# Weight sums of a Strassen MLP made during attention: 48 pieces of 192 columns in the first 24 chunks, in place of 72 pieces of 128 columns in all 36

## The chip, the cores and the metric

The kernel runs on one core of a Trainium2 chip. The metric is the device time of one execution in microseconds (us), as a median over executions. The core has TensorE (PE, with its weight loads as PEld), VectorE (DVE), ScalarE (ACT), GpSimd (POOL) and SyncE (SP), which here only issues DMAs. POOL also issues DMAs of its own.

## The reference

One image of 48 x 48 tokens with 768 channels goes through a transformer block and then through a Fourier block (AFNO). Cut to what matters here:

```python
xn   = layernorm(x)
qkv  = xn @ qkv_w + qkv_b                        # 12 heads of 64 channels
attn = softmax(q*scale @ k.T + rel_h + rel_w)    # 2304 x 2304 for each head
x    = x + (attn @ v) @ proj_w + proj_b
h    = gelu(layernorm(x) @ mlp_w1 + mlp_b1)      # 3072 hidden channels
x    = x + h @ mlp_w2 + mlp_b2
x    = x + irfft2(blockwise_mlp(rfft2(x)))       # AFNO
```

## The kernel before

All matmuls are in float32. The dense layers are computed in Strassen-Winograd form: a product of two-by-two blocks is made of seven block products instead of eight. For that, sums of the weight blocks are needed. With the blocks a11, a12, a21, a22 of a weight, the helper `left` (L164 to L167) makes four 128 x n sums or differences, three into new tiles and one in place; `right` (L175 to L178) does the same for the other operand. The MLP weights `mlp_w1` and `mlp_w2` are turned into such sets of seven while attention runs, and the results are kept in DRAM (`w1_d`, `w2_d`) until the MLP reads them.

**Attention.** Heads go in pairs (`pr`, 6 of them), queries in chunks of 384 (`c`, 6 of them), so there are 36 chunks. In a chunk, PE makes the scores of 18 key tiles for both heads (`content`, L678, and `position`, L687), ACT takes the exponential into `exps` (L697, tile `main`), DVE adds the exponentials up in `pairs` (L871), then `acc` (L875). Then PE makes the products with the values in six thirds (`products`, L710). Between those thirds the list `between` puts other work:

- third 1: `asked`, then `denominators` on DVE (transpose L728, reduction into `part` L730);
- third 4: `inverses`: PE sums `part` over partitions (L739, one matmul ahead of the rest of the products), DVE takes the reciprocal into `rden` (L741) and adds to `sums` (L742), POOL adds `rden` to `inverse` (L743). `rden` has two buffers;
- third 5: SP stores `rden` to DRAM (`left_apart`, L757), stores earlier outputs (`stored`, L791), reads the denominators back to all partitions (L770). DVE scales the output of the chunk two before (`scaled`, L782, tile `o`, two buffers), and POOL adds the bias of the values to it (L785).

SP also issues 24 small DMAs for each chunk that fill `terms` (L317 and L321), read by L687.

**The weight sums.** `sum_jobs` lists 72 jobs: 12 hidden chunks, two weights, three pieces of 128 columns. A job takes three steps on POOL, all through one tile `seven` with a single buffer:

```python
nc.gpsimd.dma_start(out=seven[:, :4], in_=(w1_blocks, w2_blocks)[k][n, i])   # L802, in asked
(left, right)[k](nc.gpsimd, ...)                                             # four sums, in summed
nc.gpsimd.dma_start(out=to, in_=seven)                                       # L815, in summed
```

`asked` is called twice in a chunk (at key tile 2 and in third 1) and `summed` twice (at key tile 12 and after the chunk's last product), so a chunk takes two jobs and the 72 jobs fill the 36 chunks. As `seven` has one buffer, the load of the next job waits until the store of the one before has landed. POOL works through its instructions in order, so the `inverse` addition and the bias addition of a chunk stand behind the jobs that are ahead of them.

**After attention.** DVE adds up `sums` and `inverse` (L1005, L1006) to a flag that says whether the softmax without a maximum was safe (L1008, L1010; PE turns it with L1028), makes the weight sums of the projection (L919), and then takes the projection's products as they come. The first two token tiles are projected plainly (`plainly`, PE L933, DVE L937), the next ones by seven products (`projected`, PE L957, DVE L970, L975, L979, POOL L967). The sums of the attention output that these need are made on DVE (`ogs`, L175 to L178). POOL adds the bias of the projection to the 18 tiles of the residual (`residual`, L896). Then a branch on the flag (L1044, L1045), the rest of the projection, the MLP (L1320, L1378, reading `w1_d` and `w2_d` at L1302 and L1305), and AFNO.

The order on PE, SP, ACT, DVE and POOL is the written one within each of these stages.

Of the kernel before, what the change touches and what calls it, by code (L numbers as in the profile page):

```python
# [10 lines left out]
F32 = mybir.dt.float32  # L11
# [8 lines left out]
P = 128  # L20
# [7 lines left out]
FF = 4 * C  # L28
FCH = 256
# [5 lines left out]
CH = C // 2  # L35
# [12 lines left out]
def block_then_afno(  # L48
# [27 lines left out]
    nc = tc.nc  # L76
# [18 lines left out]
    dram = ctx.enter_context(tc.tile_pool(name="scratch", bufs=1, space=DRAM))  # L95
# [9 lines left out]
    oT = dram.tile([C, T], F32, name="oT")  # L105
    stat_d = [dram.tile([12, P], F32, name=f"stat_d{p}") for p in range(T // TB)]
    den_d = dram.tile([NC * (T // G), 2 * G], F32, name="den_d")
    w1_d = [dram.tile([P, 7, 3, P], F32, name=f"w1_d{n}") for n in range(FF // FCH)]
    w2_d = [dram.tile([P, 7, FF // (FCH * NS), CH], F32, name=f"w2_d{s}") for s in range(NS)]

    big1 = ctx.enter_context(tc.tile_pool(name="big1", bufs=1))
# [91 lines left out]
    with ExitStack() as flag_scope:  # L203
# [12 lines left out]
        with ExitStack() as att:  # L216
# [444 lines left out]
            with tc.manual_schedule(engines={mybir.EngineType.PE, mybir.EngineType.SP}):  # L661
# [6 lines left out]
                o_pool = att.enter_context(tc.tile_pool(name="att_o", bufs=2))  # L668
# [121 lines left out]
                        pr, c, o = results.pop(0)  # L790
                        queue.dma_start(out=oT[ts(pr, P), ts(c, G)], in_=o)  # L791

                sum_jobs = [(k, n, i) for n in range(FF // FCH) for k in range(2) for i in range(3)]
                in_hand = []

                def asked():

                    if not sum_jobs:
                        return
                    k, n, i = sum_jobs.pop(0)  # L800
                    seven = o_pool.tile([P, 7, P], F32, name="seven", bufs=1)
                    nc.gpsimd.dma_start(out=seven[:, :4], in_=(w1_blocks, w2_blocks)[k][n, i])  # L802
                    in_hand.append((k, n, i, seven))

                def summed():

                    if not in_hand:
                        return
                    k, n, i, seven = in_hand.pop(0)
                    (left, right)[k](  # L810
                        nc.gpsimd, *(seven[:, a] for a in range(4)), [seven[:, a] for a in (4, 5, 6)]
                    )
                    s, j = divmod(n, FF // (FCH * NS))
                    to = w2_d[s][:, :, j, ts(i, P)] if k else w1_d[n][:, :, i]
                    nc.gpsimd.dma_start(out=to, in_=seven)  # L815

                def between(pr, c, acc):

# [28 lines left out]
                with tc.manual_schedule(  # L847
# [4 lines left out]
                    for pr in range(NC):  # L852
                        for c in range(T // G):
# [4 lines left out]
                            if c == 4 and pr == NC - 1:  # L858
                                nc.sync.dma_start(
                                    out=pw, in_=proj_w.rearrange("(c p) f -> p c f", p=P)  # L860
                                )
                            pairs = o_pool.tile([P, 2, 2, G], F32, name="pairs", bufs=1)
                            for kt in range(NT):
                                if kt == 2:
                                    asked()
                                elif kt == 12:
                                    summed()
                                scores(pr, c, kt, exps[:, kt])
                                if kt > 2 and kt % 2:
                                    so_far = exps[:, ds(0, 2)] if kt == 3 else pairs  # L870
                                    nc.vector.tensor_tensor(  # L871
                                        pairs, so_far, exps[:, ds(kt - 1, 2)], ALU.add
                                    )
# [4 lines left out]
                            for i in range(6):  # L878
                                for what in work.get(i, ()):
                                    what()  # L880
                                products(op, heads[pr][2], range(3 * i, 3 * i + 3))
                            finish(pr, c, op)
                            summed()
                    scaled(0)
                    stored(nc.gpsimd)
# [102 lines left out]
        with tc.tile_pool(name="ps_flag", bufs=1, space=PSUM) as psum, tc.tile_pool(  # L988
            name="ps_early", bufs=1, space=PSUM
# [55 lines left out]
        with tc.If(safe < 1):  # L1045
            with ExitStack() as att:
                xnT = main.rearrange("p (c t) -> p c t", c=NC)
                with tc.tile_pool(name="g_ln1", bufs=3) as ln1, tc.tile_pool(
                    name="g_ps_ln1", bufs=2, space=PSUM
# [24 lines left out]
                for pr in range(NC):  # L1074
                    w3 = []
                    for n, name in enumerate(("g_wq", "g_wk", "g_wv")):
                        w = w_pool.tile([P, NC, P], F32, name=name)
                        nc.sync.dma_start(
                            out=w,
                            in_=qkv_w[:, ds(n * C + pr * P, P)].rearrange("(c p) f -> p c f", p=P),  # L1080
# [33 lines left out]
                    for sg in range(T // SG):  # L1114
# [37 lines left out]
                        for i in range(2):  # L1152
                            wp = psum.tile([P, 24, 16], F32, name="g_wp", tag="m")
                            for r in range(24):
                                w = i * 24 + r
# [15 lines left out]
                        for j in range(2):  # L1171
                            for qt in range(SG // P):

                                s = p_pool.tile([P, T], F32, name="s")
# [25 lines left out]
                                for kg in range(NT // 3):  # L1200
# [20 lines left out]
                                    out=oT[ds(pr * P + 64 * j, 64), ds(sg * SG + qt * P, P)],  # L1221
                                    in_=ot[rows, :],
                                )
            with tc.tile_pool(name="g_ps_proj", bufs=2, space=PSUM) as psum, tc.tile_pool(
                name="g_og", bufs=2
# [17 lines left out]
        with tc.tile_pool(name="ps_proj", bufs=1, space=PSUM) as psum, tc.tile_pool(  # L1243
            name="ps_turn", bufs=2, space=PSUM
        ) as psum_turn, tc.tile_pool(name="proj_late", bufs=2) as pl:
            hats, ogs = [], {EARLY: sums_of_outputs(pl, kept[EARLY])}
            for u in range(EARLY, PAIRS):
# [5 lines left out]
                n = u - EARLY  # L1253
# [29 lines left out]
    with ExitStack() as mlp:  # L1283
# [15 lines left out]
        def weights(p, n):  # L1299

            w = wpool.tile([P, 7, 3, P], F32, name="w1")
            nc.sync.dma_start(out=w, in_=w1_d[n])  # L1302
            v = wpool.tile([P, 7, CH], F32, name="w2")
            g, j = divmod(n, FF // (FCH * NS))
            nc.sync.dma_start(out=v, in_=w2_d[g][:, :, j])  # L1305
            ready_w[p, n] = w, v

        def hidden(p, n):
# [29 lines left out]
            nc.scalar.copy(m1, bank[0])  # L1338
            product(1, s2, t2, True)
            u = summed(bank[1], m1, "u")  # L1340
            yield
            product(2, a21, t3, True)
# [93 lines left out]
        def turned(piece):  # L1436

            for i in range(4 * piece, 4 * piece + 4):
# [6 lines left out]
                )  # L1445

        weights(0, 0)
        for p in range(T // TB):
            for n in range(n_f):
                if (p, n) == (0, 2):  # L1450
                    nc.sync.dma_start(out=b2, in_=mlp_b2[0, :].partition_broadcast(P))
                    nc.sync.dma_start(out=rows_dft, in_=c_rows)
                work = hidden(p, n)
                for i in range(3):
                    next(work)
                    if n:
                        added(p, n - 1, i)
                if n < n_f - 1 and (p == 0 or n):
                    weights(p, n + 1)
                if p < 2 and 4 <= n < 10:  # L1460
                    normalised(p + 1, n - 4)
            for i in range(3):
                if p < 2:
                    turned(i)
                added(p, n_f - 1, i)
            if p < 2:
                sums_of_tokens(xt, xs)
                for n in range(2):
                    weights(p + 1, n)
            rows_forward(p)  # L1470
        in_order.close()

    with ExitStack() as sp:
# [35 lines left out]
        for t in range(2):  # L1509
            nc.sync.dma_start(  # L1510
                out=d2[ts(t, HW)].rearrange("p n o -> p (n o)"),
                in_=fb2[t, :].partition_broadcast(HW),
# [272 lines left out]
def _laid_out(x, given):  # L1785

    import numpy as np

    w = {name: np.asarray(a) for name, a in given.items()}

    def columns(v):
        return v.reshape(-1, P).T

    vecs = np.concatenate(
        [
            columns(v)
            for v in (
                w["L0_conv_ln1_g"],
                w["L0_conv_ln1_b"],
                w["L0_conv_ln2_g"],  # L1800
                w["L0_conv_ln2_b"],
                w["L0_conv_qkv_b"],
                w["L0_conv_mlp_b1"],
            )
        ],
        axis=1,
    )

    rel = np.zeros((HD, 2, 112), np.float32)
    for i, name in enumerate(("L0_conv_rel_pos_h", "L0_conv_rel_pos_w")):  # L1810
        rel[:, i, : 2 * HW - 1] = w[name][::-1].T
    n_s, n_j = NS, FF // (FCH * NS)
    arrays = {
        "x": np.asarray(x).reshape(T, C),

        "x_blocks": np.asarray(x).reshape(6, 8, 3, 16, C).transpose(0, 2, 1, 3, 4).reshape(T, C),
        "x_turned": np.asarray(x).reshape(6, 8, 3, 16, C).transpose(4, 0, 2, 1, 3).reshape(C, T),
        "qkv_w": w["L0_conv_qkv_w"],
        "proj_w": w["L0_conv_proj_w"],
        "w1_blocks": w["L0_conv_mlp_w1"]  # L1820
        .reshape(2, 3, P, n_s, 2, n_j, P).transpose(3, 5, 1, 2, 4, 0, 6)
        .reshape(n_s * n_j, 3, P, 4, P),
        "w2_blocks": w["L0_conv_mlp_w2"]
        .reshape(n_s, 2, n_j, P, 2, 3, P).transpose(0, 2, 5, 3, 1, 4, 6)
        .reshape(n_s * n_j, 3, P, 4, P),
        "vecs": vecs,
        "v_b": w["L0_conv_qkv_b"][None, 2 * C :],
        "proj_b": w["L0_conv_proj_b"][None],
        "mlp_b2": w["L0_conv_mlp_b2"][None],
        "rel": rel,  # L1830
        "fw1": w["L1_conv_w1"].transpose(2, 0, 1, 3),
        "fb1": w["L1_conv_b1"].transpose(2, 0, 1),
        "fw2": w["L1_conv_w2"].transpose(2, 1, 0, 3),
        "fb2": w["L1_conv_b2"].reshape(2, -1),
    }
    return {name: np.ascontiguousarray(a) for name, a in arrays.items()}
# [24 lines left out]
```

## Time and profile before

| what | value |
|---|---|
| time, median of 3 runs | 2864.15 us (2859.18 to 2873.69) |
| the profiled execution's own time | 2856.51 us |
| its span, first to last instruction | 2854.7 us |
| mean granted TensorE clock | 0.993 |
| attention: first POOL job to last product | about 403 to 1419 us of the span |
| projection up to the branch | about 1419 to 1503 us |
| busy in 402 to 1420: PE, DVE, ACT, POOL | 1012.91, 697.53, 621.88, 467.34 us |
| busy in 1420 to 1462: PE, DVE, ACT, POOL | 26.57, 17.42, 0.48, 22.61 us |

A row of a group of instructions reads: line, engine, operation, output and input tiles with their shapes, how many; then busy time and mean of one in ns; then idle time of the engine before them and what ended it. A row of the waits reads: engine, tile and line that waited, what released it; then us in total, times, longest. A row of a timeline reads: start, duration, engine, line, operation, tiles, count, and in brackets the idle time before it and what ended that. Times are from the start of the span.

### The profile page before, as it was taken

What the parts mean: (1) busy time and instruction counts of PE and PEld (TensorE: products, weight loads), DVE (VectorE), ACT (ScalarE), POOL (GpSimd) and SP (SyncE); (2) the same over time, 40 slices, a digit from 0 to 9 for tenths busy, and PEclk for the clock granted to TensorE, in tenths of its full rate; (3) what the DMA queues carried; (4) which work ended last, traced back from release to release, by engine and by line L of the source; (5) the groups of instructions that cost most, each with busy time, mean ns of one, the idle gap of its engine ahead of it and who ended that gap; (6) DMA issues with size and microseconds to landing.
All of it is one profiled execution on the core that took longest, in us unless ns stands there. A gap on an engine that the chain in (4) does not pass through costs nothing. (4 is left out here: it accounts for less than half of the span.)

```text
span 2854.7 us, 41104 instructions
## 1 busy us (share of the span) xinstructions
PE 2795.7 (98%) x15759; PEld 1719.4 (60%) x15759; DVE 1719.9 (60%) x2520; ACT 920.0 (32%) x1466; POOL 804.8 (28%) x806
## 2 busy tenths in 40 slices
PE   8999999999999999999989999999999999999999
PEld 4555656665656565656545555555555555556887
DVE  5434246767676676767546665675565566566665
ACT  1101126666656575756401211021011211112332
POOL 3505124444445344444573100020000100002432
PEclk9999999999999999999989999999999999999999
DMA  4535387485875858677453232332232322233254
GB/s 154 177 104 168 101 170 164 105 171 124 145 179 117 173 122 164 139 141 138 136 181 111 75 116 78 116 132 73 111 116 78 141 97 102 92 107 111 61 161 141
DMA packets 233405, 363.47 MB, mean 127 GB/s; under 512 B 26948, under 2 KB 203964, under 8 KB 227056
## 3 DMA queue, kind: packets, MB, share of 16 engines
q1 hardware_dynamic: 215720, 306.80, 40.7%
q0 software_dynamic: 15040, 52.11, 6.1%
q8 instruction: 127, 2.08, 0.3%
q10 hardware_dynamic: 2440, 1.84, 0.2%
q14 instruction: 78, 0.64, 0.1%
HBM read 211.59 MB, written 85.35 MB: 104 GB/s over the span
## 5 line engine op out<-in xcount | busy, mean ns | idle before, releaser
L697 ACT ACTIVATE main<-sp 128x768 f32<-128x768 f32 x648 | 516.4, 812 | 34.5 <-PE sp L687 19.3
L1320 PE MATMUL h<-shared,w 128*128 128x384 f32 x1512 | 504.1, 486 | 0.7 <-issue 0.7
L871 DVE TENSOR_TENSOR pairs<-pairs,main 128x1536 f32<-128x1536 f32 x252 | 456.9, 1813 | 27.1 <-DVE pairs L871 0.9
L687 PE MATMUL sp<-terms,select 64*128 64x384 f32 x1296 | 412.3, 629 | 0.0
L1320 PEld LDWEIGHTS h<-shared,w 128*128 128x128 f32 x1512 | 287.0, 190 | 202.0 <-issue 2.5
L1380 DVE TENSOR_TENSOR main<-o,main 128x384 f32<-128x384 f32 x540 | 299.1, 557 | 38.3 <-PE o L1378 0.2
L1395 POOL TENSOR_TENSOR main<-main,acc 128x384 f32<-128x384 f32 x9 | 11.4, 1263 | 924.5 <-DVE main L1380 665.3
L678 PE MATMUL sp<-shared 64*128 64x384 f32 x1296 | 264.9, 485 | 1.6 <-ACT row_hi L249 1.0
L678 PE MATMUL sp<-qT,kT 64*128 64x384 f32 x1296 | 264.5, 484 | 0.0
L1378 PE MATMUL o<-w,hs 128*128 128x384 f32 x648 | 262.5, 487 | 1.5 <-DVE hs L165 1.0
L1378 PE MATMUL o<-w,hT 128*128 128x384 f32 x648 | 245.1, 487 | 3.0 <-DVE main L1380 3.0
L710 PE MATMUL op<-main,shared 128*64 128x384 f32 x1296 | 218.0, 488 | 0.0
L710 PE MATMUL op<-main,v 128*64 128x384 f32 x1296 | 217.2, 488 | 0.0
L1326 ACT ACTIVATE hT<-c,vec 128x384 f32<-128x384 f32 x108 | 66.5, 615 | 465.1 <-DVE c L1332 465.1
L871 DVE TENSOR_TENSOR pairs<-main 128x1536 f32<-128x1536 f32 x36 | 64.0, 1778 | 221.5 <-ACT main L697 221.4
L1332 DVE TENSOR_TENSOR c<-h,u 128x384 f32<-128x384 f32 x108 | 60.2, 557 | 212.9 <-PE h L1320 212.9
L1378 PEld LDWEIGHTS o<-w,hT 128*128 128x128 f32 x648 | 122.7, 190 | 90.2 <-DVE main L1380 6.3
L1378 PEld LDWEIGHTS o<-w,hs 128*128 128x128 f32 x648 | 122.5, 190 | 89.5 <-DVE main L1380 4.9
L687 PEld LDWEIGHTS sp<-terms,select 64*128 64x128 f32 x1296 | 125.5, 186 | 83.6
L537 PE MATMUL m<-main 128*128 128x384 f32 x504 | 164.2, 487 | 2.1 <-DVE main L187 1.6
L710 PEld LDWEIGHTS op<-main,v 128*64 128x64 f32 x1296 | 97.3, 137 | 92.4 <-issue 67.7
L710 PEld LDWEIGHTS op<-main,shared 128*64 128x64 f32 x1296 | 96.5, 137 | 89.3 <-issue 64.4
(205 smaller groups left out, 3807.3 us busy)
## 6 DMA issues: line engine op xcount, KB each, us to landing
w<-w_d SPq DMA_DIRECT2D x72, 1344.0 KB
w_d<-seven POOLq DMA_DIRECT2D x72, 448.0 KB, 4.6
terms<-col_parts SPq DMA_DIRECT2D x432, 72.0 KB
seven<-in_w_blocks_dram POOLq DMA_DIRECT2D x72, 256.0 KB, 4.4
terms<-row_hi SPq DMA_DIRECT2D x216, 72.0 KB
terms<-row_lo SPq DMA_DIRECT2D x216, 72.0 KB
main<-in_qkv_w_dram SPq DMA_DIRECT2D x36, 384.0 KB
z<-zt SPq DMA_DIRECT2D x48, 192.0 KB
```

The lines of the kernel that those rows point to most:

```text
L537: nc.tensor.matmul(bank, a[:, c, :], b[:, c, :], start=(first and c == 0), stop=(c == 2), skip_group_check=not first,)
L678: nc.tensor.matmul(sp[:, j, :G], kT[at, ts(kt, P)], qT[at, ts(c, G)], start=first, stop=not first,)
L687: nc.tensor.matmul(sp[:, j, :G], select[at, a % 2], ready[pr, c][at, a // 2, b], start=first, stop=not first,)
L697: nc.scalar.activation(p, sp[:, :, :G], AF.Exp, scale=HD**-0.5)
L710: nc.tensor.matmul(op[ts(j, 64)], v[:, kt, ts(j, 64)], exps[:, kt, j, :], start=(kt == 0), stop=(kt == NT - 1),)
L871: nc.vector.tensor_tensor(pairs, so_far, exps[:, ds(kt - 1, 2)], ALU.add)
L1320: nc.tensor.matmul(bank[i], a[:, c, :], b[:, c, :], start=(start and c == 0), stop=(c == 2), skip_group_check=not start,)
L1326: nc.scalar.activation(h[:, i, ts(k, G)], src, AF.Gelu, bias=col(V_B1 + tiles_of_chunk(n)[i]))
L1332: nc.vector.tensor_tensor(t, src, other, ALU.add)
L1378: nc.tensor.matmul(bank[k], a, b, start=start, stop=True, skip_group_check=not start)
L1380: nc.vector.tensor_tensor(dst, bank[k], dst, ALU.add)
L1395: nc.gpsimd.tensor_tensor(x12, x12, acc[i], ALU.add)
```

## The change

A job has 192 columns instead of 128. There are two pieces for each weight chunk instead of three, so 48 jobs; still two in a chunk, so the list is empty after 24 chunks. A load moves 384 KB instead of 256 KB, a store 672 KB instead of 448 KB; the four sums run over 128 x 192 elements. The weights are laid out for that in the input arrays, and `w1_d` is kept as 7 x 384 columns for each partition; the MLP reads the same bytes in the same order as one run per partition. The tile `seven` grows by 7 x 64 x 4 = 1792 bytes per partition.

```diff
-    w1_d = [dram.tile([P, 7, 3, P], F32, name=f"w1_d{n}") for n in range(FF // FCH)]
+    w1_d = [dram.tile([P, 7, CH], F32, name=f"w1_d{n}") for n in range(FF // FCH)]
...
-                sum_jobs = [(k, n, i) for n in range(FF // FCH) for k in range(2) for i in range(3)]
+                sum_jobs = [(k, n, i) for n in range(FF // FCH) for k in range(2) for i in range(2)]
...
-                    seven = o_pool.tile([P, 7, P], F32, name="seven", bufs=1)
+                    seven = o_pool.tile([P, 7, CH // 2], F32, name="seven", bufs=1)
...
-                    to = w2_d[s][:, :, j, ts(i, P)] if k else w1_d[n][:, :, i]
-                    nc.gpsimd.dma_start(out=to, in_=seven)
+                    to = w2_d[s][:, :, j] if k else w1_d[n]
+                    nc.gpsimd.dma_start(out=to[:, :, ts(i, CH // 2)], in_=seven)
...
-            nc.sync.dma_start(out=w, in_=w1_d[n])
+            nc.sync.dma_start(out=w.rearrange("p a c f -> p a (c f)"), in_=w1_d[n])
...
-        .reshape(2, 3, P, n_s, 2, n_j, P).transpose(3, 5, 1, 2, 4, 0, 6)
-        .reshape(n_s * n_j, 3, P, 4, P),
+        .reshape(2, 3, P, n_s, 2, n_j, P).transpose(3, 5, 2, 4, 0, 1, 6)
+        .reshape(n_s * n_j, P, 4, 2, CH // 2).transpose(0, 3, 1, 2, 4),
...
-        .reshape(n_s, 2, n_j, P, 2, 3, P).transpose(0, 2, 5, 3, 1, 4, 6)
-        .reshape(n_s * n_j, 3, P, 4, P),
+        .reshape(n_s, 2, n_j, P, 2, 2, CH // 2).transpose(0, 2, 5, 3, 1, 4, 6)
+        .reshape(n_s * n_j, 2, P, 4, CH // 2),
```

Here P is 128 and CH is 384.

## The prediction

> **What bounds the kernel now.** I read the page first: PE is busy in 98% of the span, POOL in 28%.
>
> ```profile
> PE 2795.7 (98%) x15759; PEld 1719.4 (60%) x15759; DVE 1719.9 (60%) x2520; ACT 920.0 (32%) x1466; POOL 804.8 (28%) x806
> ```
>
> So work taken off POOL gains nothing by itself. What counts is where PE waits, and whether POOL is behind that. The table of waits, read next, has POOL as the releaser in one long wait only, and POOL itself waits mostly for its own DMAs:
>
> ```profile
> POOL seven L802 <- DMA w_d<-seven: 301.2, 71, 8.4
> POOL seven L164 <- DMA seven<-in_w_blocks_dram: 99.6, 31, 9.7
> POOL seven L175 <- DMA seven<-in_w_blocks_dram: 88.0, 33, 5.4
> DVE total L1006 <- POOL inverse L743: 28.3, 1, 28.3
> ```
>
> A job is thus a serial chain (load, wait, four sums, store, wait), and at the end of attention DVE waits 28.3 us for POOL's last `inverse`. The timelines show why: POOL is a chunk late. In chunk 3 of 36, PE's denominator product (L739) is at 481.08 and POOL's `inverse` at 481.84. In the last chunk PE's is at 1414.82, POOL's at 1444.04, a lag of 29 us:
>
> ```profile
> 481.08 0.19 PE L739 MATMUL small<-gather,part 128*48 128x32 f32 x1
> 481.84 0.53 POOL L743 TENSOR_TENSOR inverse<-inverse,rden 24x32 f32<-24x32 f32 x1 [2.23 <-DVE sums L742]
> 1414.82 0.19 PE L739 MATMUL small<-gather,part 128*48 128x32 f32 x1
> 1444.04 0.27 POOL L743 TENSOR_TENSOR inverse<-inverse,rden 24x32 f32<-24x32 f32 x1
> ```
>
> PE pays for this lag after attention, in PE's timeline behind its last product (1414.89 + 4.06 = 1418.95):
>
> ```profile
> 1414.89 4.06 PE L710 MATMUL op<-main,v 128*64 128x384 f32 x23
> 1423.68 18.25 PE L933 MATMUL m<-col_parts,og 128*128 128x384 f32 x48 [4.73 <-DMA og<-oT]
> 1445.63 0.27 PE L1028 MATMUL line<-ident,both 128*1 128x128 f32 x1 [3.69 <-DVE both L1010]
> 1449.62 3.71 PE L957 MATMUL m<-col_parts,og 128*128 128x384 f32 x6 [3.72 <-DVE main L937]
> 1457.67 4.21 PE L957 MATMUL m<-pws,ogs 128*128 128x384 f32 x6 [4.33 <-DVE ogs L176]
> 1461.67 2.73 PE L957 MATMUL m<-col_parts,og 128*128 128x384 f32 x6
> ```
>
> Inside attention PE loses almost nothing today, but with no reserve. DVE ends `part` (L730) at 1413.75 + 0.95 = 1414.70, and PE uses it at 1414.82. A DVE that comes later stops PE.
>
> **What the Trainium skill says.** (1) "SBUF — State Buffer", section "SBUF: two separate sides": a DVE instruction with two SBUF inputs and a POOL instruction that reads SBUF exclude each other for a whole instruction. The trace agrees: a sum of 128 columns takes 443 to 460 ns alone and up to 2.0 us when an L871 addition (1.76 us) is under way, and L871 takes 1.757 us at least, 1.823 in the median. (2) "DMA: Bandwidth & Descriptors", section "Anatomy of one DMA — SWDGE (gpsimd) path": a POOL DMA takes about 2.0 us plus bytes/436e3. For 256 KB this gives 2.6 and for 448 KB 3.05; the trace has at least 2.7 and 3.6, and 4.4 and 4.6 in the median, where DMAs of SP compete. (3) "PSUM — Partial Sum Buffer", section "Engine vs sequencer instructions": queues of POOL and DVE are strict first in, first out. The trace agrees: `inverse`, ready at 1415.4, runs behind the jobs at 1444.04.
>
> **Part 1, a longer job.** Today, from the rows by form: load issue 0.56, wait for the load 187.6/72 = 2.61, four sums 311.0/72 = 4.32, gap 0.40, store issue 0.93, wait for the store 301.2/71 = 4.24: 13.1 us. Two jobs, `inverse` 0.52 and bias 1.34 make 28.0 us a chunk, beside PE's chunk of (1419.01 - 430.14)/35 = 28.25 us (ends of chunks by ACT's copy L751). With waits for DVE (50.7/36 = 1.4) POOL needs slightly more than PE, hence the lag.
>
> With 192 columns:
>
> - Sums: 128 x 384 takes 1130 ns (L164 on `main`), 128 x 128 at least 443, so 2.7 ns a column: 64 columns in four sums add 0.69 us, alone or behind DVE.
> - Load: by the skill's rate at least 131072/436e3 = 0.30; at most half of what lies over the fixed 2.0, (4.4 - 2.0)/2 = 1.2. I take 0.5.
> - Store: at least 229376/436e3 = 0.53, at most (4.6 - 2.0)/2 = 1.3. I take 0.85. Both stand nearer the low end: part of the surplus is waiting in the queue, which bytes do not lengthen. The issues (0.56, 0.93) keep their number of rows; I leave them.
>
> A job gets 2.04 us longer (1.5 to 3.2), so a chunk's POOL work is 28.0 + 4.1 = 32.1 us against 28.25. The lag grows by 3.83 us a chunk, 88 us over the 23 chunks up to the last with jobs.
>
> **How much lag is free.** Behind POOL's jobs stand `inverse` and the bias addition. DVE's L741 of chunk c needs the `rden` buffer of c-2 (two chunks, 56.5 us), and L782 needs an `o` whose bias addition stood in POOL's queue at c-2 and which SP has then stored. Between L741 and the next L871 DVE has 8.3 us (1388.28 to 1396.56), 1.6 of it work, so 6.7 to spare. By `rden` the limit is 56.5 + 6.7 = 63 us. By `o` it is 56.5 + 7.7 - 1.6 for bias and issue - 5.5 for landing (L791 on POOL's queue) = 57. I use 57. Past that DVE starts `pairs` late, `part` is late, and PE waits at L739, with the products and the next chunk's scores behind it. SP, stuck in L791, holds `terms` back as well, but those are issued chunks ahead. The stall is 88 - 57 = **+31 us**. With both ends: 3.2 to a job gives 23 x 6.15 - 57 = 84, and 1.5 gives 23 x 2.75 - 57 = 6.
>
> **Part 2, DVE beside longer sums.** L871 loses 0.066 us to a sum of 128 columns. 64 more hold the port some 0.14 us longer. The mean of a sum, 1.08 us between 0.45 and 1.9, says that some 43% of eight a chunk collide: 0.5 us a chunk on DVE. In about half of 24 chunks there is no reserve: **+4 us** (2 to 8). Gone in the last 12 chunks: under 1 us.
>
> **Part 3, the end.** Without jobs in the last 12 chunks POOL has 1.9 us of work a chunk and catches up at once. `inverse` follows L739 within 1 us as in chunk 3, L1006 runs at about 1416, flag and L919 are done by 1421, and L937 meets each product as it comes. SP's L791, today stuck until 1418.36 for POOL's L785 of 1417.08, goes early, and `og` is there when the last product ends. PE then runs 18.25 us of L933 from 1419, the transpose, two products of 1.94, and stands at 1441.5 where it stands now at 1461.67: **-20 us**. If `og` still arrives at 1423.7, it is -15.5. What is late next: L896, paced by L967 and so by PE, moves along; the wait at the branch (3.89 us) stays.
>
> **Without cost:** the MLP's weight reads (same bytes, same runs), the larger tile, 96 DMA issues instead of 144, 192 sums instead of 288 (POOL is not PE).
>
> **Sum.** 31 + 4 - 20 = +15 us on 2856.51, the profiled execution, 2871.5. Its time lies 7.6 under the median of 2864.15, so **2879 us**.
>
> **Rivals.** *Faster:* the lag stays below 57, there is no stall, and only the end is seen: 4 - 20 = -16, 2848 us. It decides at a job longer by (57/23 + 0.25)/2 = 1.36 us; the sums and the skill's least DMA times already give 1.52, so DMA growth would have to be hidden or the free lag nearer 65. For it speaks that today's POOL held a lag of 30 without cost. *No change:* the job grows by 1.5 to 2.0, the stall is 6 to 29 and mostly cancels the end: 2854 to 2877. *Much slower:* the DMAs grow with bytes in full, +68, 2932. *It does not do what it says:* POOL clears late but the end is bound by SP's reload of the denominators (an 8.9 us wait) and not by POOL; then the end gives little and the stall stays, near 2895.
>
> **Chances.** Within 0.5% (14 us; about what a measurement of this kernel can tell from no change) 0.27; slower 0.50, with the last two rivals in it; faster 0.23. Range 2847 to 2910: from the faster rival to a job 2.7 us longer (stall 61, +45).
>
> **What would show it.** Right: L743's lag behind L739 grows by about 4 us a chunk to some 55 to 60 by chunk 16, then PE waits at L739 for L730 by about 4 us a chunk until chunk 24; chunks 25 to 36 take 28.2 us; L1006 no longer waits; L933 to the third L957 without gaps. Job sums of 0.62 us alone, landings of 4.9 (load) and 5.4 (store). Wrong: the lag levels off under 57 with no waits at L739 (the faster rival), or chunks slow down before the lag is there (DVE beside POOL was underpriced).

## The result and the profile after

The changed kernel takes **2882.3 us** (median of 20 runs, 2871.1 to 2889.3), the kernel before 2864.1 (20 runs beside it, 2855.0 to 2876.8). The ratio is 1.0056 with a 95% interval of 1.0043 to 1.0070: slower by 18 us, where 2879 was forecast (15 us slower). The profiled executions lie further apart, 2885.64 against 2856.51 us, because the one of before lies 7.6 us under its median and the one of after 3.4 us over. All sums below are on the profiled executions: +29 us.

The page has POOL with less work and PE with the same:

```profile
PE 2797.0 (97%) x15759; PEld 1717.5 (60%) x15759; DVE 1723.1 (60%) x2520; ACT 920.0 (32%) x1466; POOL 694.3 (24%) x662
```

POOL lost 110 us of busy time and the kernel got slower. In the table of waits POOL still waits for the two DMAs of each job (columns: us in total, times, longest), now 47 times instead of 71 but 5.2 us each instead of 4.2 for the store. The line of L1006, where DVE waited 28.3 us for POOL after attention, is gone:

```profile
POOL seven L802 <- DMA w_d<-seven: 245.0, 47, 10.0
POOL seven L175 <- DMA seven<-in_w_blocks_dram: 82.9, 23, 7.6
POOL seven L164 <- DMA seven<-in_w_blocks_dram: 82.5, 23, 6.7
```

The timelines of PE and POOL show the lag. In the last chunk with jobs (number 23, counted from 0, as everywhere from here on) PE's L739 is at 1115.11 and POOL's L743 of the same chunk at 1181.56, 66 us later, where the kernel before had 21. In the last chunk of attention POOL is 1.6 us behind, where it was 29:

```profile
1115.11 0.19 PE L739 MATMUL small<-gather,part 128*48 128x32 f32 x1
1181.56 0.27 POOL L743 TENSOR_TENSOR inverse<-inverse,rden 24x32 f32<-24x32 f32 x1
1467.25 0.19 PE L739 MATMUL small<-gather,part 128*48 128x32 f32 x1
1468.85 0.56 POOL L743 TENSOR_TENSOR inverse<-inverse,rden 24x32 f32<-24x32 f32 x1
```

PE's timeline behind attention has no gap left. From the end of the last product (1467.32 + 4.06 = 1471.4) to the third L957 it is 20.2 us, where it was 42.7:

```profile
1467.32 4.06 PE L710 MATMUL op<-main,v 128*64 128x384 f32 x23
1471.97 15.75 PE L933 MATMUL m<-col_parts,og 128*128 128x384 f32 x48 [0.58 <-ACT ot L751]
1487.56 0.27 PE L1028 MATMUL line<-ident,both 128*1 128x128 f32 x1
1487.66 2.10 PE L957 MATMUL m<-col_parts,og 128*128 128x384 f32 x6
1489.60 2.10 PE L957 MATMUL m<-pws,ogs 128*128 128x384 f32 x6
1491.54 2.10 PE L957 MATMUL m<-col_parts,og 128*128 128x384 f32 x6
```

So the end gives 22.5 us. But attention's last product ends at 1471.4 instead of 1419.0, 52.4 us later. 52.4 - 22.5 = 29.9, which covers the 29.1 between the two executions. Where attention lost it is in the waits between 400 and 1475 us:

```profile
PE small L739 <- DVE part L730: 33.2, 8, 16.7
PE small L280 <- ACT col_parts L249: 10.2, 2, 5.2
ACT col_parts L249 <- DMA terms<-col_parts: 11.3, 2, 5.8
DVE o L782 <- DMA spread<-den_d: 74.8, 13, 19.6
DVE rden L741 <- POOL inverse L743: 20.3, 5, 5.3
SPq L791 <- POOL o L785: 127.2, 13, 25.4
```

PE waits mainly for `part`, as forecast, but not by 4 us in each chunk. From one ACT copy L751 to the next, five chunks come as lumps: 7, 15, 19, 21 and 25 are 4.6, 7.7, 12.7, 7.7 and 18.9 us longer than their kind in the kernel before, 51.6 together. The others are at most 1.1 us longer than they were, and chunk 13 is 2.4 shorter. In chunks 7, 19 and 25 PE waits for `part`; in 15 and 21 it waits for ACT's L249, which waits for SP's DMAs out of `col_parts` (second and third line). And the last line names a waiter that the forecast had set aside: SP, which issues its DMAs in order, stands 127 us at the store L791 for POOL's bias addition L785.

How this becomes a stall is seen ahead of chunk 25, in SP's, DVE's and PE's timelines:

```profile
1116.40 0.33 SPq L791 DMA_DIRECT2D oT<-o  x1
...
1160.96 1.13 SPq L770 DMA_DIRECT2D spread<-den_d  x2
1166.97 0.56 DVE L782 TENSOR_TENSOR o<-ot,spread 128x384 f32<-128x384 f32 x1 [19.56 <-DMA spread<-den_d]
1187.59 0.26 PE L739 MATMUL small<-gather,part 128*48 128x32 f32 x1 [16.68 <-DVE part L730]
```

SP has stood at L791 since 1105.5 and gets past it at 1116.4, with POOL. It then issues 48 DMAs for `terms` back to back, 0.6 us or more each, and reaches the loads of `spread` 45 us later, though what they read (the denominators of chunk 22) was stored by L757 at 1105.0. They are issued 73.4 us after that chunk's `rden`; in the kernel before it was 58.0 us, and in e4_both_on_dve below, where SP does not wait for POOL, it is 60.0. DVE, also in order, stands at L782 for 19.6 us with `pairs` and `part` of the next chunk behind it, and PE waits 16.7 us for `part`.

### The profile page after: what moved, and what is told of

Read it like the earlier page. It is cut to its first block, busy times and chain, and to the rows that moved or that the text cites. A ratio compares the mean times of both kernels' runs of the same rounds, so it can differ in the third digit from the quotient of the medians.

```text
span 2883.8 us, 40970 instructions
## 1 busy us (share of the span) xinstructions
PE 2797.0 (97%) x15759; PEld 1717.5 (60%) x15759; DVE 1723.1 (60%) x2520; ACT 920.0 (32%) x1466; POOL 694.3 (24%) x662
## 5 line engine op out<-in xcount | busy, mean ns | idle before, releaser
L1326 ACT ACTIVATE hT<-c,vec 128x384 f32<-128x384 f32 x108 | 66.4, 615 | 465.2 <-DVE c L1332 465.1
```

The source lines that it names most:

```text
L1326: nc.scalar.activation(h[:, i, ts(k, G)], src, AF.Gelu, bias=col(V_B1 + tiles_of_chunk(n)[i]))
```

## The experiments

Theories: **backlog** (POOL's chain of jobs needs longer than PE's chunk, the lag grows until some link of the attention reaches POOL), with two candidates for the link that stops PE, **SP-queue** (L791, as just shown) and **rings** (the two buffers of `rden` and of `o`, which are used in turn, as the prediction had it); and **contention** (the bigger pieces slow DVE or the DMAs whatever POOL's lag is). "35 chunks" is the time from the first to the last L751, "lag" the time from PE's L739 to POOL's L743 of the same chunk, "end" the time from the last product to the third L957, "a job" the mean time from one L802 to the next from the third job on; these are of one profiled execution each. Each ratio is taken against runs of the kernel before that lay beside it (medians 2864.1 to 2866.9 us); the runs of a kernel number 6 to 9, 20 for the changed one, and 22 for e6 and e12. Where POOL keeps up (e3, e5, e13), "a job" shows no more than the pace at which PE's chunks ask for jobs (two in a chunk of 28.2 us are one in 14.1; in e3, four in three chunks, one in 21.2), not how long POOL's chain takes.

| kernel | median us | ratio to before (95%) | 35 chunks | lag, chunk 23 | a job | end |
|---|---|---|---|---|---|---|
| before | 2864.1 | 1 | 988.9 | 21.4 | 14.60 | 42.7 |
| after | 2882.3 | 1.0056 (1.0043 to 1.0070) | 1041.5 | 66.4 | 16.49 | 20.2 |
| e2_bias_on_dve | 2890.6 | 1.0080 (1.0052 to 1.0109) | 1045.5 | 83.6 | 16.86 | 20.2 |
| e7_rings | 2881.9 | 1.0051 (1.0032 to 1.0071) | 1035.3 | 66.2 | 16.51 | 20.2 |
| e9_store_by_pool_rings | 2882.7 | 1.0054 (1.0031 to 1.0076) | 1050.3 | 81.5 | 16.84 | 20.1 |
| e10_bias_dve_rings | 2842.8 | 0.9928 (0.9902 to 0.9955) | 990.8 | 136.1 | 17.39 | 20.2 |
| e4_both_on_dve | 2848.0 | 0.9939 (0.9914 to 0.9964) | 993.5 | none on POOL | 17.42 | 20.2 |
| e3_spread_out | 2836.3 | 0.9888 (0.9864 to 0.9911) | 991.9 | 0.8 | 21.39 | 20.2 |
| e13_no_sums | 2836.9 | 0.9899 (0.9879 to 0.9920) | 993.8 | 0.8 | 14.37 | 20.2 |
| e5_before_two_buffers | 2829.9 | 0.9874 (0.9848 to 0.9901) | 984.0 | 0.8 | 14.10 | 20.2 |
| e6_before_inverse_on_dve | 2862.4 | 0.9996 (0.9980 to 1.0011) | 1002.3 | none on POOL | 14.76 | 33.8 |
| e12_before_both_on_dve | 2862.1 | 0.9994 (0.9980 to 1.0009) | 983.9 | none on POOL | 14.78 | 56.9 |

### One link cut: e2, e7, e9

**e2_bias_on_dve** takes the link to SP out:

```diff
-                        nc.gpsimd.tensor_scalar(o, o, col(V_VB + pr), None, ALU.add)
+                        nc.vector.tensor_scalar(o, o, col(V_VB + pr), None, ALU.add)
```

> The changed kernel with one edit: the bias of L785 runs on VectorE instead of POOL, so that the store of L791, which SyncE issues in order, no longer waits for POOL. Baseline: the changed kernel at 2882 us, its profile with attention's last product at 1471.4 us (1419.0 before the change). Theory SP-queue (POOL's lag reaches the products through SyncE, which stands at L791 for POOL's bias and so sends `spread` and the pair's `terms` late): the lumps of chunks 7, 15, 19, 21 and 25 (51 us together) go, VectorE gets some 0.4 us a chunk more; 2882 - 51 + 5 to 10 = 2835 to 2843 us, and L791's wait for POOL in the attention window falls from 127 us to none. Theory rings (the lag stops at some 57 to 63 us because `rden` and `o` have two buffers): POOL's job-filled chunk falls from about 32.5 to 31 us, the lag at the last such chunk from 66 to about 35 us, no stall either: the same 2835 to 2843. Theory contention (the bigger pieces slow VectorE and the DMAs whatever POOL's lag is): unchanged or slower, 2880 to 2890.

It is no faster than the changed kernel, and SP-queue alone is refuted: SP no longer waits for POOL at all, and the 35 chunks still take 1045.5 us. The waits say what took over:

```profile
DVE rden L741 <- POOL inverse L743: 118.7, 11, 20.4
PE small L739 <- DVE part L730: 37.8, 8, 11.1
```

Now the ring of `rden` holds DVE, as the prediction had it, at a lag of 61 to 84 us from chunk 12 on. The other half of the expectation failed too: with the bias gone, POOL's job did not get shorter (16.86 us for 16.49). In the changed kernel L785 runs while POOL would otherwise wait for a load of its job, as at 1181.79 in the timeline (behind a load's issue at 1180.99), which is a likely reason why taking it away does not shorten the chain.

**e7_rings** lengthens the rings and leaves SP as it is:

```diff
-                    rden = o_pool.tile([ND, 32], F32, name="rden")
+                    rden = o_pool.tile([ND, 32], F32, name="rden", bufs=4)
...
-                        o = o_pool.tile([P, G], F32, name="o")
+                        o = o_pool.tile([P, G], F32, name="o", bufs=3)
```

> The changed kernel with `rden` in four buffers instead of two and `o` in three instead of two; nothing else. Theory rings: the limit of the lag moves from some 60 to 85 us (the third `o`: one chunk of 28 us more), 28 us of the stalls go: about 2855 us, and the lag of L743 behind L739 climbs past 80 us. Theory SP-queue: SyncE stands at L791 for POOL just as before, so the stalls stay or grow and the lag may climb a little higher: 2878 to 2895 us. Theory contention: 2882 us.

2881.9 us: rings alone is refuted as well. The lag stays at 66 us in chunk 23, and in the table of waits SP's is the one of the changed kernel:

```profile
SPq L791 <- POOL o L785: 126.7, 13, 26.2
PE small L739 <- DVE part L730: 26.2, 6, 12.5
```

**e9_store_by_pool_rings** adds to e7 that POOL issues the store itself (`def stored(queue=nc.gpsimd)` instead of `nc.sync`).

> The changed kernel with the rings of e7_rings, and with the store of L791 issued by POOL itself behind its bias, so that SyncE never waits for POOL in the attention; POOL gets about 1 us more a chunk (L815's issue takes 0.93 us), and so lags some 5 to 6 us a chunk instead of 4 to 5. Theory SP-queue: no lumps at the pairs' starts; the lag climbs freely to the new limit of about 85 us near chunk 16 and from then on the products stall by 5 to 6 us a chunk for some 7 chunks: -51 + 30 to 40 = 2860 to 2872 us; where the rings hold longer (the lag reaching 110 us or more) 2832 to 2845. Theory rings: 2855 to 2870 with e7_rings the same. Theory contention: 2882 us or more.

2882.7 us, again no gain and outside what SP-queue gave. SP is free, `rden` has four buffers, and now DVE stands at L782, thirteen times in a row (for the outputs of chunks 11 to 23), 148 us in all. The table of waits names no releaser or POOL's sums for nearly all of them. The landings in the trace name it: each of the thirteen L782 starts 0.07 to 0.08 us after POOL's store of the output three before has landed. That is the ring of `o` with its three buffers, which POOL's late store frees. The last of them:

```profile
1199.18 0.56 POOL L791 DMA_DIRECT2D oT<-o  x1
1204.02 0.56 DVE L782 TENSOR_TENSOR o<-ot,spread 128x384 f32<-128x384 f32 x1 [16.89 <-issue]
```

The store landed at 1203.94. PE's wait for `part` is 49.0 us. Each time the lag stops somewhere between 58 and 84 us, at a different link.

### All links cut, or no lag: e10, e4, e3

If the links are nearly equally long, cutting one shows nothing, and cutting all must show everything. **e10_bias_dve_rings** is e2 with six buffers for `rden`.

> The changed kernel with both links by which POOL's backlog could reach the products taken out at once: the bias of L785 on VectorE (as in e2_bias_on_dve, whose stalls stayed, with 119 us of VectorE's L741 waiting for POOL's L743) and `rden` in six buffers, so that L741 waits for the L743 of six chunks before, not two. The 48 jobs stay as they are, two in each of the first 24 chunks. Theory backlog (one lag on POOL, several links of nearly the same length: cut one and the next one holds): the lag climbs freely to 100 to 125 us at chunk 23, no wait for POOL appears on VectorE or SyncE, attention's last product ends at 1420 to 1432 us instead of 1471, and the time is 2832 to 2845 us. Theory contention (pieces of 192 columns slow VectorE or the DMAs by themselves): stalls remain in the chunks with jobs, 2870 us or more.

2842.8 us, as the backlog theory said, 39 us under the changed kernel, with the same 48 jobs in the same 24 chunks. The lag grows to 136 us, more than the 100 to 125 expected, and of the long waits of PE this is left:

```profile
PE small L739 <- DVE part L730: 4.1, 6, 1.5
```

Neither the bias on DVE alone (e2) nor longer rings alone (e7) gives anything; the bias on DVE with the longer ring of `rden` gives 39 us. **e4_both_on_dve** leaves POOL only the jobs (L743 and L785 both on `nc.vector`):

> The changed kernel with the bias of L785 and the flag's sum of L743 both on VectorE: POOL has nothing left in the attention but the 48 jobs, and nothing of the attention waits for POOL. Theory backlog: as e10_bias_dve_rings, 2832 to 2845 us; the jobs still take 32 to 34 us a chunk and end near 1185 to 1215 us, but nothing waits for them. Theory contention: 2870 us or more.

2848.0 us, 3 us over the range expected, but again far from the 2870 or more of contention, and the 35 chunks take 993.5. The jobs need 34.8 us a chunk here (2 x 17.42), more than expected, and it does not matter.

**e3_spread_out** leaves all links and takes the lag away: a counter makes every third `asked` return at once, so that the 48 pieces of 192 columns fill the 36 chunks.

```diff
+                asks = [0]
...
-                    if not sum_jobs:
+                    asks[0] += 1
+                    if asks[0] % 3 == 0 or not sum_jobs:
                         return
```

> The changed kernel with one edit: every third call of `asked` does nothing, so the 48 jobs of 192 columns are spread over all 36 chunks (four in three chunks, where the changed kernel has six). POOL then has 1.33 x 15.1 + 1.5 + 0.4 = 22 us of work in a chunk of 28.2. Both theories of a lag (SP-queue and rings): the lag never grows past some 5 us, attention ends where it ended before the change or a little earlier (1415 to 1422 us), and the last pieces are done in chunk 35, so the gain at the end stays: 2882 - 50 = 2832, up to 2843 us. Theory contention by the bigger pieces: same pieces, same bytes, so the loss stays: 2870 to 2885 us.

2836.3 us, within the range. The lag is 0.8 us in chunk 23 and never over 1.4, and the end is as short as with the last 12 chunks empty. So the gain at the end does not need the jobs to be over early; it needs POOL to be on time. And it is the pace of the jobs in the first 24 chunks, not their size, that makes the changed kernel the slower one.

### What the bigger pieces cost by themselves: e13

**e13_no_sums** replaces the four sums of a job by one operation, so the sums are left out and the three blocks are stored as zeros:

```diff
-                    (left, right)[k](
-                        nc.gpsimd, *(seven[:, a] for a in range(4)), [seven[:, a] for a in (4, 5, 6)]
-                    )
+                    nc.gpsimd.memset(seven[:, 4:], 0.0)
```

> The changed kernel with the sums of each job left out: its four POOL operations on `seven` are replaced by one that fills the three blocks of sums with zeros (so the outputs lack the weight sums); both DMAs of each of the 48 jobs stay, with all their bytes. A job then takes 16.5 - 5.0 + 0.3 to 1 = 12 to 12.5 us, two of them 24 to 25 us a chunk of 28.2, with the bias inside the waits. Theory backlog: no lag, no stall: attention's last product ends at 1414 to 1420 us and the time is 2828 to 2838 us. Theory contention by the DMAs of the bigger pieces (1.31 MB of traffic to and from DRAM in two thirds of the chunks): 2865 us or more. Contention of VectorE with POOL's long sums shows as the difference to e10_bias_dve_rings and e4_both_on_dve: 5 to 8 us less in attention's end than their 1423 to 1424.

(The traffic named there should be 384 + 672 KB, 1.08 MB a job.) The time, 2836.9, is as the backlog theory said, and the lag stays under 10 us. The finer expectations failed. A job takes 14.1 us from the issue of its load to the landing of its store, not 12 to 12.5, and attention's last product ends at 1425.2, not at 1414 to 1420. The 35 chunks take 993.8 us, no less than with the sums (990.8 in e10, 993.5 in e4, 991.9 in e3), while the pieces of 128 columns take 983.9 in e12 and 984.0 in e5. So 7 to 10 us of attention go with the pieces of 192 columns even where little or nothing waits for POOL, and they stay when the sums are gone. These are single executions, but the medians of e3 and e13 lie as far over that of e5 (6 and 7 us), with the same end. The largest piece of it in e4, where nothing of the attention waits for POOL, is this wait in chunk 7:

```profile
626.65 0.20 PE L739 MATMUL small<-gather,part 128*48 128x32 f32 x1 [2.72 <-DVE part L730]
```

DVE had stood 9.6 us for `spread` ahead of it, where it stood 6.2 in e12. That speaks against DVE and POOL sharing SBUF, and for the DMAs, but the stalls of e13 fall into other chunks than those of e4, and no run separates the size of the load from that of the store. What the cause is stays open.

### The kernel before has the same fault: e5, e6, e12

**e5_before_two_buffers** is the kernel before with

```diff
-                    seven = o_pool.tile([P, 7, P], F32, name="seven", bufs=1)
+                    seven = o_pool.tile([P, 7, P], F32, name="seven", bufs=2)
```

> The kernel before (72 pieces of 128 columns, two in each of 36 chunks) with one edit: `seven` in two buffers, so that the load of a job no longer waits for the store of the job before it. Each job then costs POOL about 0.6 + 0.9 + 4.3 to 5 us of its own work and little waiting, some 15 us a chunk of 28.2. Theory backlog: POOL's lag (30 us at the last chunk) is gone, attention's end stays at 1419 us less 1 to 3, and the tail after it shrinks from 42.7 to about 20 us as it did in the changed kernel: 2864 - 20 to 25 = 2839 to 2846 us. If what shrank the tail in the changed kernel was only that no job lies near the end, and not POOL's lag: 2855 to 2864.

2829.9 us, better than expected and **the fastest of all**, 1.3% under the kernel before. The load of a job now lies beside the sums and the store of the job before it, POOL never waits for `w_d<-seven`, and its lag stays under 5 us. Attention has no stall of PE, and behind it there is no gap:

```profile
1411.12 4.06 PE L710 MATMUL op<-main,v 128*64 128x384 f32 x23
1415.77 15.75 PE L933 MATMUL m<-col_parts,og 128*128 128x384 f32 x48 [0.58 <-ACT ot L751]
1431.36 0.27 PE L1028 MATMUL line<-ident,both 128*1 128x128 f32 x1
1431.46 2.10 PE L957 MATMUL m<-col_parts,og 128*128 128x384 f32 x6
```

The Trainium skill, page "Trainium Kernel Development and Optimization", section "Best Practices", has the plain rule to double-buffer so that DMA lies beside computing; here it is worth 35 us on an engine that is busy in 29% of the span. Two buffers of 192 columns were not run.

**e6_before_inverse_on_dve** and **e12_before_both_on_dve** asked what in POOL's lag costs the kernel before its time (L743 on `nc.vector`; in e12 L785 too).

> The kernel before with one edit: the flag's sum of L743 on VectorE, so that the flag (L1006 and what follows it) no longer waits for POOL's last jobs, while the last biases of L785 and the rows of `oT` that the first L933 products read stay behind them. If the flag's chain is what held the tail of the kernel before: 2864 - 12 to 20 = 2844 to 2852 us. If the late `og` (4.7 us ahead of L933) and the flag held it in equal parts: about 2855 to 2860.

> The kernel before (72 pieces of 128 columns, one buffer, two in each of 36 chunks) with the flag's sum of L743 and the bias of L785 both on VectorE: nothing of the attention waits for POOL any more, while the 72 jobs stay as they are and still end behind the attention's last product. In e6_before_inverse_on_dve only L743 was moved and the time stayed (2862 us), with SyncE still standing 121 us at L791 for POOL's bias and a stall of 14.8 us in chunk 34. Theory backlog (the rest of the kernel's loss is the bias, by SyncE): the stalls of the products and the wait for `og` go, 2864 - 20 to 30 = 2834 to 2846 us. If the loss is in the jobs' own DMAs and sums beside the tail (they end near 1455 us): 2850 to 2862 us.

Neither gains, and both expectations of a gain failed. In e6 the end shrinks by 9 us, and attention loses 13 in the one execution profiled: SP waits 121 us at L791 (42 in the kernel before), and PE stalls 14.8 us in chunk 34. Why SP waits longer there stays open. In e12 attention is free of stalls (983.9 us), but the end takes 56.9 us, because there is one more link behind POOL's jobs, the bias of the residual (L896), for which DVE's L937 waits:

```profile
DVE main L937 <- POOL main L896: 38.8, 1, 38.8
PE m L957 <- DVE main L937: 29.8, 1, 29.8
```

The last store of a job is issued at 1457.70, and only then come the four additions L896. As in the changed kernel, cutting links one by one moves the wait to the next one. What removed it here was a shorter chain of jobs (e5), as fewer jobs in a chunk did for the pieces of 192 columns (e3).

## Why the prediction was right, and where not

Time and direction were right, 2879 for 2882.3; the likeliest mechanism was right in outline: a POOL lag that the first 24 chunks build up, reaching PE by DVE's `part`, against a gain at the end. By its steps:

- **A longer job, +2.04 us.** Somewhat too small. By the prediction's own rows the wait for the load went from 2.61 to 3.45 us, the four sums from 4.32 to 4.85, the wait for the store from 4.24 to 5.21: +2.34, where 0.5, 0.69 and 0.85 were forecast. Landings have medians of 4.7 and 5.6 us (4.9 and 5.4 forecast). The Trainium skill's rate in "DMA: Bandwidth & Descriptors", section "Anatomy of one DMA — SWDGE (gpsimd) path", gave the lower ends of load and store, 0.30 and 0.53; the prediction stayed near them because part of the time over the rate would be waiting in the queue. Beside SP's DMAs the waits grew by 0.84 and 0.97.
- **POOL's chunk, 28.0 becoming 32.1 us.** Too small as well, by 0.7 us. POOL's L743 of chunk 23 comes 755.1 us after that of chunk 0, 32.8 a chunk. That is 105 us over 23 chunks of 28.25, where 88 were forecast; the longer job is 14 of these 17 us. The reason given for the lag of the kernel before was misread: of the 50.7 us of waits put down to DVE, 15.4 lie ahead of the first job and 23.0 ahead of L743 in chunks 0 to 6, where POOL is on time and merely waits its turn. The lag grows after that, from chunk 7 to 35 at 29.0 us of POOL against 28.3 of PE.
- **Free lag, 57 us.** The size was nearly right: the lag stands between 58 and 72 us from chunk 12 to 23, and 105 - 52 = 53 us of it cost PE nothing. The place was not. The prediction put it down to `rden` and `o`, and dismissed SP with "those are issued chunks ahead". SP was the first link in the changed kernel, and by `spread` as well as `terms`. e2 and e9 show that the rings were the next ones, at 61 to 84 us, which is why the size came out.
- **Stall, +31, and DVE beside longer sums, +4.** Together 35 forecast, 52.4 measured. The 17 us of lag that the forecast lacked are as much as the difference. The stall is not a steady 4 us from chunk 16 on, but five lumps, the first in chunk 7. This first one (4.6 us) is not shown to be the backlog's: the lag is only 35 us there, and e4, where nothing of the attention waits for POOL, has 2.9 us in the same chunk. Of the +4: the bigger pieces do cost 7 to 10 us where nothing else stalls, but e13 says that the sums on DVE's port are not the reason.
- **The end, -20.** Right: -22.5, with all four gaps ahead of the third L957 gone, in every kernel whose POOL is on time at the end. The other 2.5 us are L933, which the prediction left at 18.25 us and which takes 15.75 with no gap ahead of it.
- **Sum.** +15 forecast, +29 between the profiled executions, +18 between the medians. The stall was 17 us too small and the gain at the end 2.5. That the time came out within 3 us is partly luck: the profiled executions, on which the sum was made, lie 11 us further apart than the medians.

The faster rival (lag below 57, no stall) and the one of SP's reload at the end fall with the trace. The rival of no change falls too: the stall is over the 29 us that it allowed, and the time over its 2877. The much slower one needed DMAs that grow fully with their bytes; their landings grew by 0.3 and 1.1 us in the median.

## What to carry to other kernels

An engine that is 24% busy can set the time if it works through a serial chain of DMA, sums and DMA in order: compare the time of the chain for one iteration, from issue to issue in its timeline where that engine is late (where it is on time, the interval only shows the pace of the others), with that of the engine that bounds, and shorten the chain (two buffers, or fewer jobs in an iteration) before cutting what hangs on it. When a backlog is bounded by several links of nearly one length, removing any one of them can show nothing, as in e2, e7 and e9, and this is no evidence against the backlog; remove all, or the backlog itself. A DMA queue issued in order is such a link: one store that waits for a late engine holds back every load behind it.

## What was not expected of the hardware

A stall of PE can cost more than its length. After a wait of 1.5 us (e10), 2.4 us (before) or 2.7 us (e4) the next 40 matmuls of a chunk take 6.3 us. After waits of 2.5 to 16.7 us, seen in the changed kernel and e2, they take 7.8 to 9.1, and after one of 2.0 us in e3 they take 8.0. So between 2 and 3 us the length of the wait alone does not decide. In the timeline of the changed kernel, after the 16.7 us shown above, 23 products take half as long again as the 4.06 us of a chunk without a stall:

```profile
1187.74 6.04 PE L710 MATMUL op<-main,shared 128*64 128x384 f32 x23
```

The Trainium skill, "TensorE: Matmul & The Clock Gate", section "Part 1: The HAM clock gate (the "warmup" mystery)", says that the array falls to half its clock after an idle window of about 3.4 us, on a window that runs freely. The traces agree in kind, with products of 128 x 384 following each other at 0.64 instead of 0.33 us after a gap. They differ in the length: waits of 2.0 us (e3) and 2.5 us (e2) were enough. The five lumps of the changed kernel add up to 51.6 us, and the waits at their heads to 40.6 (2.7, 5.0, 11.0, 5.2 and 16.7), so at most 11 of the 52 us are this.

The times of the kernels with a backlog scatter: the fastest and the slowest run lie 28 us apart in the kernel before (27 runs beside e12), 18 in the changed kernel (20 runs) and 18 in e10 (8 runs), but 5 in e5 and 3 in e3 (6 runs each). And a job is slower when nothing stalls: 17.4 us in e10 and e4 against 16.5 in the changed kernel. There PE, DVE and SP stand still for a part of the time, which may be the reason; no run shows it.
